# Expert lists: the compared places stored with four tiles innermost instead of eight

## The chip, the cores and the metric

The kernel runs on one core of one Trainium2 chip. The metric is the device time of one execution in microseconds (us); less is better. Three runs of the kernel before took 1474.82, 1474.82 and 1475.46 us, so the median is 1474.82 us. Engines are named as in the profile: PE (matrix multiplication), PEld (PE's loading of weights), DVE (vector), ACT (scalar activation), POOL (the general-purpose engine, which also issues indirect DMAs) and SP (which issues the other DMAs).

## The reference, cut to what matters

A tensor of 4 x 1024 tokens with 256 values each passes four sublayers, each as `x + layernorm(sublayer(layernorm(x)))`: a gated attention in groups of 64, a low-rank feed-forward, an attention with 16 heads whose weights are relu(scores), and a mixture of eight experts. Only the last one matters here:

```python
def _L1_ffn_ref(x, Wg, W1, b1, W2, b2):
    ...
    k = min(max(int(n * C / e), 1), n)          # 4096 * 2 / 8 = 1024 tokens an expert
    xt = x.reshape(n, h)
    S = jax.nn.sigmoid(xt @ Wg).T               # 8 x 4096 scores
    G, I = jax.lax.top_k(S, k)
    ex = xt[I]
    hid = jax.nn.gelu(jnp.einsum('ekh,ehf->ekf', ex, W1) + b1[:, None, :], approximate=False)
    out = (jnp.einsum('ekf,efh->ekh', hid, W2) + b2[:, None, :]) * G[..., None]
    new_x = jnp.zeros_like(xt).at[I.reshape(-1)].add(out.reshape(-1, h))
```

Each expert takes the 1024 tokens with its highest scores. The kernel has to turn the scores of an expert into a list of 1024 token numbers before it can gather the tokens.

## The kernel before, in words

The first three sublayers take the first 963 us and are left alone. What follows is the expert stage.

**Sizes.** P = 128 partitions; the 4096 tokens are NTILE = 32 tiles of 128, one token of each tile on each partition; an expert's list is NC = 8 chunks of 128; QT = 8 tiles are a quarter of the 32. An expert's 1024 tokens are worked on in two halves (`u` counts halves, 0 to 15) of 512.

**How a list is made** (class `List`; one object for each of the eight experts, steps run in this order). `Search` finds by bisection the score of the 1024th token. `sort` marks tokens above and at it; `rank` counts, with matmuls against triangular ones and scans, which place each chosen token has in the list, and splits the place into a chunk (`hi`) and a position within the chunk (`lo`, one bf16 number for each partition and tile; a token that is not chosen matches no position). `chunks` (L1934 to L1942) compares `hi` with the eight chunk numbers and makes `pair`: for each tile 16 columns, eight with the token's partition number and eight with its tile number. `places` (L1960 on) compares `lo` with the 128 positions: for a quarter of the tiles, one DVE instruction (L1966) writes for each partition, position and tile a bf16 one or zero into the tile `at`. The constant `each` holds the 128 positions in the form that `lo` has; before, it holds them once for each of the 32 tiles, so that the operand for a quarter is a slice of it. The first two quarters go to buffers of a pool (name `at`), the last two into space that the tile `x` no longer needs (`in_stored`, so their name in the profile is `x`). `collect` (L1976) then runs one matmul for each of the 32 tiles: weights are the 16 columns of `pair` of that tile, the moving operand is the 128 positions of that tile out of `at`. Before, the eight tiles of a quarter are innermost in `at`, so position p of one tile lies 8 elements, 16 bytes, behind position p - 1. Tile j adds into output partitions 32 (j % 4) to 32 (j % 4) + 15, so that four tiles in a row use four different groups of rows. ACT copies the sums (`listed`, L1985), and `gather` (L1988, L1990) adds the four groups with one more matmul, turns the result into the integers `idx`, and has POOL issue eight indirect DMAs (`got`, L2000) that fetch the tokens.

**What the experts do.** `turn` transposes the gathered tokens on PE (L2170). Experts 0, 1, 2 and 7 run plain matmuls (`feed_forward`, L2285), experts 3 to 6 a form with seven products in place of eight (`feed_forward_by_seven`, L2231, with additions on DVE at L2246, L2248, L2250, L2257 and L2260 between the products and weight sums on POOL at L2195). `project_back` (L2311) multiplies back; DVE adds the bias (L2326) and scales (L2327) into one of four buffers `y`, and POOL adds the rows to the result in memory with an indirect DMA (L2328), each of which waits until the one before has landed. The next pair of weight matrices is loaded by SP while an expert runs.

**What sets the order.** PE, DVE and ACT run in the order in which the program is written; nothing is reordered. The list of expert 0 is made first, with nothing beside it but short idle matmuls (L203). The steps of the other lists stand in an agenda and are taken one at a time between the matmuls of the experts (`go_on_with_lists`), when a counter of estimated time allows it; the estimates are constants in the code. So every list but the first has its 32 matmuls of `collect` in the middle of the matmuls of some expert.

Of the kernel before, what the change touches and what calls it, by code (L numbers as in the profile page):

```python
# [12 lines left out]
BF16 = mybir.dt.bfloat16  # L13
AF = mybir.ActivationFunctionType
# [5 lines left out]
P = 128  # L20
# [54 lines left out]
def kernel(  # L75
# [32 lines left out]
    nc = tc.nc  # L108
# [3 lines left out]
    NTILE = NT // P  # L112
# [109 lines left out]
    with ExitStack() as st1:  # L222
# [96 lines left out]
        for r in range(2):  # L319
            for j in range(4):  # L320
                at = 32 * j + HD * r
# [124 lines left out]
        wk = st1.enter_context(tc.tile_pool(name="l0", bufs=2))  # L446
# [12 lines left out]
        def later_counts():  # L459
            r = {}  # L460

            def count_int(name, shape, pattern, per_partition, tag=None, base=0):
                n_i = const.tile(shape, I32, tag=tag or name, name=name, bufs=3 if tag else 1)
                nc.gpsimd.iota(n_i, pattern=pattern, base=base, channel_multiplier=per_partition)
                return n_i

            def count(name, shape, pattern, per_partition, dtype, base=0):
                n_i = count_int(f"{name}_i", shape, pattern, per_partition, "whole", base)
                r[name] = const.tile(shape, dtype, name=name)
                nc.gpsimd.tensor_copy(r[name], n_i)  # L470

            count("count_p", [P, P], [[1, P]], 0, BF16, 1)
            count("count_c", [P, NC], [[1, NC]], 0, BF16)
            count("count_t", [P, NTILE], [[1, NTILE]], 0, BF16)
            count("in_tile", [P, 1], [[0, 1]], 1, F32)
            r["bits0"] = count_int("bits0", [P, NVAL], [[1, NVAL]], 0)
            r["ahead_i"] = count_int("ahead_i", [P, P], [[1, P]], -1, "whole")

            quads = r["quads"] = const.tile([P, 2 * NC], F32, name="quads")
            nc.gpsimd.tensor_tensor(quads, ident[:, 0 : 2 * NC], ident[:, 32 : 32 + 2 * NC], ALU.add)
            for q in (2, 3):
                nc.gpsimd.tensor_tensor(quads, quads, ident[:, 32 * q : 32 * q + 2 * NC], ALU.add)
            return r
# [525 lines left out]
        for t in range(NB):  # L1011
# [4 lines left out]
            if t == 0:  # L1016
                whole = later_counts()
            elif t == 1:
                mb1, all_b, upto_b, bits, fold = later_constants(whole)
                count_p, count_c, count_t, in_tile = (  # L1020
                    whole[name] for name in ("count_p", "count_c", "count_t", "in_tile")
                )
# [29 lines left out]
            while main:  # L1052
                on_pe(*main.pop(0))
                if not beside and hidden and len(main) % 2 == 0:
                    for step in (hidden.pop(0) for _ in range(min(2, len(hidden)))):
                        on_pe(*step)
                places = max(len(main) - len(hidden), 0) + 1
                for _ in range(-(-len(beside) // places)):
                    on_pe(*beside.pop(0))
# [44 lines left out]
    with ExitStack() as st3:  # L1104

        wts = st3.enter_context(tc.tile_pool(name="l1w", bufs=6))
        wk = st3.enter_context(tc.tile_pool(name="l1a", bufs=2))
# [557 lines left out]
        while True:  # L1665
# [7 lines left out]
            at = pe[0]  # L1673
# [76 lines left out]
    with ExitStack() as st4:  # L1750
        keep = st4.enter_context(tc.tile_pool(name="moe_keep", bufs=1))
# [27 lines left out]

        weights = [load_expert(0), load_expert(1)]  # L1780

        each = keep.tile([P, P, NTILE], BF16, name="each")
        behind_exp = mybir.DependencyInfo(mybir.DependencyClass.Sync, mybir.DependencyReason.DATA)
        whole = nc.scalar.activation(each, count_p.unsqueeze(2).to_broadcast([P, P, NTILE]), AF.Copy, scale=-1.0 / P)
        tc.add_manual_dep(whole.ins, state["exp"].ins.name, behind_exp, reason="the last scores go ahead")

        whole_c = keep.tile([P, NC], F32, name="whole_c")
# [9 lines left out]
        wk = st4.enter_context(tc.tile_pool(name="moe", bufs=2))  # L1797
        ps = st4.enter_context(tc.tile_pool(name="moe_ps", bufs=2, space=PSUM))
        QT = NTILE // 4
# [81 lines left out]
        def in_stored(half):  # L1881

            room = xs[ADDED - 1].rearrange("p j d -> p (j d)")[:, half * TB : (half + 1) * TB]
            return room.bitcast(BF16).rearrange("p (a b) -> p a b", b=QT)

        class List:

# [72 lines left out]
            def places(self, part):  # L1960
                js = slice(part * QT, (part + 1) * QT)
                if part < 2:
                    self.at[part] = wk.tile([P, P, QT], BF16, tag="at", name="at", bufs=2)
                else:
                    self.at[part] = in_stored(part - 2)
                nc.vector.tensor_tensor(  # L1966
                    self.at[part],
                    self.lo[:, js].unsqueeze(1).to_broadcast([P, P, QT]),
                    each[:, :, js],
                    ALU.is_equal,  # L1970
                )

            def collect(self, part):
                for j in range(part * QT, (part + 1) * QT):
                    u = 32 * (j % 4)
                    nc.tensor.matmul(  # L1976
                        parts[u : u + 2 * NC, 0:P],
                        lhsT=self.pair[:, j, :, :].rearrange("p v c -> p (v c)"),
                        rhs=self.at[part][:, :, j - part * QT],
                        start=(j < 4),  # L1980
                        stop=(j >= NTILE - 4),
                    )
                if part == 3:
                    self.listed = wk.tile([P, P], BF16, tag="listed", name="listed")
                    nc.scalar.copy(self.listed, parts[:, 0:P])  # L1985
# [443 lines left out]
```

## Time and profile before

| | us |
|---|---|
| median of three runs | 1474.82 |
| lowest, highest | 1474.82, 1475.46 |
| the profiled execution, its time | 1478.4 |
| the profiled execution, span of its instructions | 1476.6 |
| busy PE, DVE, ACT, POOL (of the span) | 1418.0, 868.6, 738.4, 531.3 |
| DVE compares of `places` (L1966), 32 | 20.6 busy |
| PE matmuls of `collect` (L1976), 256 | 17.8 busy |
| ACT writing the constant `each` (L1784), one | 3.60 |

The profiled execution is one execution on the chip with a record of each instruction; times of single instructions are from it. In a timeline row the first number is the start, the second how long the group was busy, then engine, line, operation, output <- inputs, partitions x elements and type, and in brackets how long the engine had been idle and what ended that. In a group's row the numbers behind the bar are busy time in all, mean ns of one instruction, then idle time ahead of it. Matmuls are pipelined, so one starts long before the one ahead of it ends: how many fit into a time is read from their starts. PEclk, the clock that the throttle granted to PE, is 1.00 in nearly all of the expert stage.

### The profile page before, as it was taken

How to read it: one execution, taken by the hardware profiler on the slowest of the kernel's cores; microseconds unless marked ns; L12 is line 12 of the kernel's file. 1: busy time of each engine (PE TensorE's matmuls, PEld its weight loads, DVE VectorE, ACT ScalarE, POOL GpSimd, SP SyncE). 2: the span in 40 equal slices, each digit the busy share in tenths (PEclk: the TensorE clock that was granted, in tenths of full speed). 3: DMA queues.
4: the chain of work that ended last, by engine and by line, in shares of the span. 5: the costliest groups of instructions: out<-in, count | busy, mean ns of one | idle time of the engine just before them, and what ended most of it. 6: DMA issues, size and time to landing. Idle time of an engine off the chain costs nothing. (4 is left out here: it accounts for less than half of the span.)

```text
span 1476.6 us, 26427 instructions
## 1 busy us (share of the span) xinstructions
PE 1418.0 (96%) x10392; PEld 861.1 (58%) x10392; DVE 868.6 (59%) x2134; ACT 738.4 (50%) x1013; POOL 531.3 (36%) x662
## 2 busy tenths in 40 slices
PE   8999999999899999999999999849999998999997
PEld 4666666667544545544555458527666665756674
DVE  5456655576554648565765677774536765355246
ACT  4244555444368887788778788422211232232142
POOL 4023231232352324342333123422344333553655
PEclk9999999999999999999999999969999999999999
DMA  8400000002643482456246430241333323343364
GB/s 221 138 1 1 1 1 1 1 0 83 203 122 97 122 249 76 146 163 195 83 119 209 135 87 19 90 122 22 101 73 80 75 65 54 73 101 58 73 167 132
DMA packets 104854, 138.76 MB, mean 94 GB/s; under 512 B 25470, under 2 KB 64795, under 8 KB 104603
## 3 DMA queue, kind: packets, MB, share of 16 engines
q1 hardware_dynamic: 74512, 81.75, 18.0%
q0 software_dynamic: 30160, 55.32, 16.1%
q8 instruction: 81, 1.33, 0.4%
q14 instruction: 43, 0.34, 0.1%
q10 hardware_dynamic: 58, 0.01, 0.0%
HBM read 75.29 MB, written 61.51 MB: 93 GB/s over the span
## 5 line engine op out<-in xcount | busy, mean ns | idle before, releaser
L1705 ACT ACTIVATE w<-sc 128x1024 f32<-128x1024 f32 x394 | 378.9, 1024 | 61.4 <-PE sc L1528 60.7
L1549 PE MATMUL po<-w,vaug 128*17 128x256 f32 (+1 forms) x4608 | 255.9, 358 | 0.9 <-DVE turned L1607 0.6
L2311 PE MATMUL py<-w,hid 128*128 128x256 f32 x1024 | 230.6, 383 | 3.3 <-DVE y L2326 3.3
L2311 PEld LDWEIGHTS py<-w,hid 128*128 128x128 f32 x1024 | 193.0, 191 | 33.8 <-issue 4.2
L1707 DVE TENSOR_SCALAR w<-sc 128x1024 f32<-128x1024 f32 x118 | 143.7, 1220 | 79.1 <-PE sc L1528 76.0
L1549 PEld LDWEIGHTS po<-w,vaug 128*17 128x17 f32 x4608 | 116.4, 97 | 117.2 <-issue 48.2
L1528 PE MATMUL sc<-q,kT 64*128 64x512 f32 (+1 forms) x1152 | 170.8, 404 | 2.9 <-ACT w L1705 1.5
L2328 POOL DMA_INDIRECT acc_d<-y,idx x56 | 88.8, 1585 | 171.1 <-issue 29.9
L1528 PEld LDWEIGHTS sc<-q,kT 64*128 64x128 f32 x1152 | 90.1, 185 | 84.1 <-issue 45.5
L2292 ACT ACTIVATE hid<-ph,mb 128x512 f32<-128x512 f32 (+1 forms) x72 | 45.8, 639 | 164.7 <-PE ph L2285 135.3
L2285 PE MATMUL ph<-xT,w 128*128 128x512 f32 (+1 forms) x288 | 114.8, 552 | 0.3 <-DVE xT L2176 0.3
L2000 POOL DMA_INDIRECT got<-tok_d,idx x64 | 66.3, 1037 | 77.9 <-DVE idx L1990 60.5
L2285 PEld LDWEIGHTS ph<-xT,w 128*128 128x128 f32 x288 | 52.6, 190 | 51.9 <-issue 48.9
L2326 DVE TENSOR_TENSOR y<-py,mb 128x256 f32<-128x256 f32 x56 | 23.6, 421 | 77.4 <-PE py L2311 50.5
L371 POOL DMA_DIRECT2D kT<-k_d x32 | 23.4, 732 | 117.0 <-PE sc L1528 53.9
L722 PE MATMUL pg<-nT,wh 128*128 128x512 f32 x128 | 60.8, 607 | 1.5 <-ACT nT L661 1.5
L848 PE MATMUL py<-wo,oT 128*128 128x256 f32 x256 | 61.6, 384 | 0.0
L738 PE MATMUL pv<-wh,nT 128*128 128x512 f32 x128 | 59.7, 592 | 0.0
L848 PEld LDWEIGHTS py<-wo,oT 128*128 128x128 f32 x256 | 47.5, 190 | 17.6 <-issue 11.0
L746 ACT ACTIVATE v<-v 128x512 f32<-128x512 f32 x32 | 20.2, 630 | 62.7 <-DVE v L745 62.7
L586 POOL TENSOR_TENSOR x<-x,y 128x1024 f32<-128x1024 f32 x13 | 30.6, 2355 | 56.4 <-ACT y L575 56.3
L1137 POOL TENSOR_TENSOR rsb<-veb,mhalf 128x1 f32<-128x1 f32 x30 | 19.7, 656 | 83.8 <-DVE veb L1136 83.8
(345 smaller groups left out, 2356.4 us busy)
## 6 DMA issues: line engine op xcount, KB each, us to landing
q<-q_d POOLq DMA_DIRECT2D x16, 1024.0 KB
kT<-k_d POOLq DMA_DIRECT2D x32, 512.0 KB
w<-in_L_ffn_W_dram SPq DMA_DIRECT2D x16, 1024.0 KB
k_d<-parts SPq DMA_DIRECT2D x48, 256.0 KB
q_d<-parts SPq DMA_DIRECT2D x48, 256.0 KB
acc_d<-logits SPq DMA_DIRECT2D x8, 512.0 KB
tok_d<-hg SPq DMA_DIRECT2D x30, 128.0 KB
x<-in_L_attn_x_dram SPq DMA_DIRECT2D x7, 512.0 KB
```

Source lines behind the costliest of these rows:

```text
L722: nc.tensor.matmul(pg, lhsT=wh[:, c, HID + e * P : HID + (e + 1) * P], rhs=d["nT"][:, c, :], start=(c == 0), stop=(c == DC - 1),)
L738: nc.tensor.matmul(pv, lhsT=d["nT"][:, c, i * P : (i + 1) * P], rhs=wh[:, c, 0:HID], start=(c == 0), stop=(c == DC - 1),)
L848: nc.tensor.matmul(py, lhsT=d["oT"][:, e, :], rhs=wo[:, e, :], start=(e == 0), stop=(e == EC - 1))
L1528: nc.tensor.matmul(sc[:, j, m * n : (m + 1) * n], lhsT=row["kT"][t, r][rows, u, (kt + m) * P : (kt + m + 1) * P], rhs=row["q"][qh, t][rows ...
L1549: nc.tensor.matmul(po[rows : rows + HD + 1, at : at + n], lhsT=row["v"][:, kt + m, HQ * t + 4 * r + 2 * u + j, :], rhs=w[:, j, (2 * m + pa ...
L1705: nc.scalar.activation(w, sc, AF.Relu)
L1707: nc.vector.tensor_scalar(w, sc, 0.0, None, ALU.max)
L2000: return nc.gpsimd.indirect_dma_start(out=dst, out_offset=None, in_=rows[:, :], in_offset=self.at_chunk(c), bounds_check=NT - 1, oob_is_er ...
L2285: nc.tensor.matmul(ph, lhsT=w1[:, c, f * P : (f + 1) * P], rhs=xT[u][:, c, h * n : (h + 1) * n], start=(c == 0), stop=(c == DC - 1),)
L2292: gelu = nc.scalar.activation(hid[:, f, h * n : (h + 1) * n], ph, AF.Gelu, bias=mb1[:, e * FC + f : e * FC + f + 1])
L2311: nc.tensor.matmul(py, lhsT=hid[:, f, i * P : (i + 1) * P], rhs=w2[:, f, :], start=(f == 0), stop=(f == FC - 1),)
L2328: scatter = nc.gpsimd.indirect_dma_start(out=acc_d[:, :], out_offset=lists[e].at_chunk(k), in_=y, in_offset=None, bounds_check=NT - 1, oob ...
```

## The change: what it does

The tile of a quarter is split into two halves of four tiles, one behind the other; in each half the four tiles are innermost. Position p of a tile now lies 4 elements, 8 bytes, behind position p - 1. The constant `each` holds every position four times instead of 32 times, and the compare uses it for both halves, by an operand with a step of zero. The count of instructions, their order on each engine and what they wait for stay as they are; the constant takes 1 KB in each partition in place of 8 KB. The same numbers are computed.

```diff
-        each = keep.tile([P, P, NTILE], BF16, name="each")
+        each = keep.tile([P, P, 4], BF16, name="each")
...
-        whole = nc.scalar.activation(each, count_p.unsqueeze(2).to_broadcast([P, P, NTILE]), AF.Copy, scale=-1.0 / P)
+        whole = nc.scalar.activation(each, count_p.unsqueeze(2).to_broadcast([P, P, 4]), AF.Copy, scale=-1.0 / P)
...
-            return room.bitcast(BF16).rearrange("p (a b) -> p a b", b=QT)
+            return room.bitcast(BF16).rearrange("p (h a b) -> p h a b", a=P, b=4)
...
-                    self.at[part] = wk.tile([P, P, QT], BF16, tag="at", name="at", bufs=2)
+                    self.at[part] = wk.tile([P, QT // 4, P, 4], BF16, tag="at", name="at", bufs=2)
...
                 nc.vector.tensor_tensor(
                     self.at[part],
-                    self.lo[:, js].unsqueeze(1).to_broadcast([P, P, QT]),
-                    each[:, :, js],
+                    self.lo[:, js].rearrange("p (h b) -> p h b", b=4).unsqueeze(2).to_broadcast([P, QT // 4, P, 4]),
+                    each.unsqueeze(1).to_broadcast([P, QT // 4, P, 4]),
                     ALU.is_equal,
                 )
...
-                        rhs=self.at[part][:, :, j - part * QT],
+                        rhs=self.at[part][:, j % QT // 4, :, j % 4],
```

## The prediction

> **What bounds the kernel now.** I read the table of stages first (one row per stretch, microseconds from the span's start; columns: length, busy time and instructions of PE, PEld, DVE, ACT, POOL, then granted clock, DMA share, GB/s), because the page's shares mix five stages and the change sits in the last one, the experts from 963 us on.
>
> ```profile
> 1040.00:1090.00 50.00, 50.00 (x200) 34.32 (x198) 28.74 (x89) 7.56 (x11) 16.60 (x12) 1.00 0.35 76
> 1090.00:1140.00 50.00, 50.00 (x239) 32.30 (x239) 23.85 (x68) 9.46 (x15) 24.90 (x21) 1.00 0.41 100
> 1190.00:1240.00 50.00, 46.15 (x213) 32.90 (x211) 26.14 (x52) 9.98 (x17) 21.43 (x17) 0.98 0.31 75
> 1300.00:1360.00 60.00, 59.82 (x272) 38.88 (x271) 29.40 (x63) 17.44 (x30) 27.44 (x21) 1.00 0.35 73
> ```
>
> The reader is to see the first busy column: PE has work all the time, DVE half of it. PE's gaps between 990 and 1445 us are 4.63 us before 1240.78, 3.35 us before 1390.75 and three under 0.4 us. So PE's instruction stream sets the end here. The chain of waits, followed back from the end, says the same and names the changed line three times (start, length, what):
>
> ```profile
> 1238.05 1.28 DVE at L1966 x2
> ...
> 1244.56 1.97 PE parts L1976 x29
> 1246.52 6.21 PE ph L2231 x14
> ...
> 1300.53 1.93 PE parts L1976 x31
> ...
> 1356.76 1.94 PE parts L1976 x32
> ```
>
> L1976 is `collect`: 32 matmuls per list that read the compared places; L1966 is `places`, the DVE compare that writes them. Next the groups of these lines by form (count, then busy us and mean ns of one), and the timeline around one `collect`:
>
> ```profile
> L1966 DVE TENSOR_TENSOR at<-lo,each 128x1024 bf16<-128x1024 bf16 x16 | 10.3, 682 | 0.0
> L1976 PE MATMUL parts<-at,pair 128*16 128x128 bf16 x128 | 8.8, 402 | 0.2 <-DVE at L1966 0.2
> L745 DVE TENSOR_TENSOR v<-pv,bhv 128x512 f32<-128x512 f32 x32 | 22.1, 690 | 27.2 <-PE pv L738 27.0
> L1549 PE MATMUL po<-w,vaug 128*17 128x256 f32 x3584 | 223.9, 383 | 0.7 <-DVE turned L1607 0.3 <-ACT w L1705 0.3
> ...
> 988.03 1.02 PE L203 MATMUL idle<-all_b 128*128 128x512 bf16 x4
> ...
> 1356.69 1.10 PE L1976 MATMUL parts<-at,pair 128*16 128x128 bf16 x16
> 1357.58 1.12 PE L1976 MATMUL parts<-x,pair 128*16 128x128 bf16 x16
> 1358.63 1.12 PE L2231 MATMUL ph<-xT,w 128*128 128x512 f32 x2
> ...
> 612.26 1.49 PE L1549 MATMUL po<-w,vaug 128*17 128x256 f32 x24
> ```
>
> The durations overlap, so starts are what to read. The four matmuls of tiles j % 4 write four groups of 32 output rows and start within 10 ns (1356.691, .694, .698, .701), the next four 0.21 us later: a list is eight waves of four. Four waves take 1357.58 - 1356.69 = 0.89 us, 0.2225 us each, for 128 columns: 1.74 ns a column. The contiguous bf16 matmuls of L203 take (1.02 - 0.38) / 3 = 0.213 us for 512 columns, 0.42 ns each. Packing four matmuls side by side is not what costs the factor of four: L1549 packs four of 256 f32 columns and needs (1.49 - 0.38) / 5 = 0.222 us a wave, what an unpacked 256-column f32 matmul also needs (16 of L2311 in 3.46 us, 0.216 us). What L1976 has and none of these has is the step: column p is read at p * 8 elements, 16 bytes on. So I read four times the contiguous price as the price of that step. Eight waves and the tail to the next matmul are 1358.63 - 1356.69 = 1.94 us a list.
>
> **The change, part by part.** Instruction order and waits are the same on all five engines; three things differ.
>
> (1) *The constant `each`* is written as 128x512 instead of 128x4096. Before: 3599 ns on ACT at 963.44. After, by an ACT row of 512 elements (L746, 630 ns): some 0.63 us, 3.0 us less. Cover: ACT has loaded its next table by 968.55 us, then idles 17.9 us for L1976; its reader on DVE comes at 983.20. Worth 0. If that cover were gone it would still be a gain.
>
> (2) *The compare* keeps 1024 elements and its bf16 operands; only the order is 2 x 128 x 4 instead of 128 x 8, and the constant is read contiguously instead of in runs of 16 bytes every 64. Its 682 ns equal the 690 ns of a 512-element f32 operation, so it handles two elements where that handles one. Best case: nothing to gain, since runs of 16 bytes already go at that rate. Worst: one element at a time, 690 + 512 x 1.04 ns (slope from 421 ns at 256 f32, L2326, to 690 at 512) = 1.22 us, 0.54 us more each. I take 0, the nearest row being the same instruction with rows twice as long; the upper end is a rival. The Trainium skill, "Vector Engine (DVE) Microarchitecture Reference", Measured stream behaviour, says that a port keeps its rate while elements come in runs of at least two adjacent 4-byte words on an 8-byte boundary; four bf16 are just that, so by it the compare stays at 0.68 us too; no row of this profile has rows so short.
>
> (3) *The matmuls' step* becomes 8 bytes. No row shows a PE read with that step, so I bound it: from below by the contiguous bf16 read, 0.42 ns a column, from above by today's 1.74 ns (nothing gained). Nothing shows a reason for a loss; the output and the weights are as before. If 16 bytes is one fetch a column and two columns now share a fetch, a column costs half, 0.83 ns, and a wave 128 x 0.83 = 0.107 us less. I take that: halving the step halves the memory covered, and the result lies between both ends. A wave is then 0.116 us; the weight loads of L1976 (mean 101 ns) go beside the wave before and hide only just; at a full-rate wave (0.2225 - 128 x 1.25 ns = 0.06 us) they would be the floor.
>
> Per list 8 x 0.107 = 0.85 us less PE time. For lists 1 to 7 (1029.9, 1090.3, 1114.3, 1194.0, 1244.5, 1300.5, 1356.7 us) PE is followed by the next `ph` matmuls without a gap, so it all counts: 7 x 0.85 = 5.95. List 0 is DVE's: its four compares come 0.60 us apart, and only the two waves after the last one (985.74 us, `listed` at 986.46) are open: 2 x 0.107 = 0.21.
>
> What is late next? `idx` of each list comes from PE and DVE and starts POOL's gathers (POOL waited 18.9 us for it at 1203.30, 2.9 us at 1365.98), and from them the serial chain of scatters (one per 4.5 us) that ends in the two PE gaps. Both chains start behind a `collect`, so gaps move along and neither grows. The stores at the end hang on the last scatter, also moved.
>
> Sum: -(5.95 + 0.21) = -6.2 us, against 1478.4 us of the profiled execution (span 1476.6, 1.8 around it), 0.42%. The median, 1474.82, lies 3.6 us below that execution; a saving in PE work carries over as it is: 1474.8 - 6.2 = **1468.6 us**. Own range 1467 to 1470.5 (a tenth of it lost or gained; weight loads as floor).
>
> A rule weighed: the Trainium skill, "SBUF — State Buffer", Specifications and the note on lines in Door 1, says that memory lines are 16 bytes, that two hits per line are needed for full bandwidth, and that eight bf16 is how far one can step for free. By the last part today's step would be free; the 1.74 ns above disagree. By the first part four innermost give two hits, thus the full rate and the fast rival below.
>
> **The rivals.**
> - *Full rate.* Two columns a fetch are enough to hide it: a column goes to 0.42 ns, a list saves 8 x 128 x 1.25 ns = 1.28 us; 7 x 1.28 + 0.32 = 9.3: 1465.5 us. Against: weight loads of 101 ns a wave would hold it at 8 x 0.12 = 0.97 a list, 1467.8.
> - *The step is not the unit.* Every column that does not touch its neighbour costs a fetch, at 8 bytes as at 16: no change, 1474.8 us. For it: 8 bytes in some 1.7 ns is just what L203 (four bf16) and L2311 (two f32, 0.84 ns a column) get, so the fetch may be 8 bytes wide. The pair granule of the skill's DVE page, cited above, would speak for it, if PE's port were alike; no run shows that.
> - *PE is not what ends last.* The scatter that lands at 1237.25 and frees `y` for DVE ends PE's 4.63 us gap. If it kept its time, lists 1 to 4 would save nothing: 3 x 0.85 + 0.21 = 2.8, 1472.1 us. Against: POOL's own 18.9 us wait for `idx` at its root.
> - *Slower: DVE loses the two at a time.* With rows of four, each compare takes 1.22 us. List 0: 4 x 0.54 = 2.15 open. Lists 5 and 7: two compares each stand before the subtraction that PE waits for (chain, 1238.05; 1352.06): 2 x 1.07 = 2.15. Together +4.3 with no gain on PE: 1479.1 us; up to 1483 if all twelve compares of lists 5 to 7 count (2.15 + 12 x 0.54 = 8.6). It decides once a compare costs more than about 0.54 x 6.2 / 4.3 = 0.8 us extra with the gain, or any 0.4 us without.
>
> **How the numbers follow.** Half price 0.52, full rate 0.14, no change on PE 0.15, chain elsewhere 0.05, slower DVE 0.14. About 0.2% (2.9 us) is what a measurement tells from no change. Half price and full rate are faster: 0.66. No change and the chain (-0.19%) are the same: 0.20. Slower: 0.14. The range reaches from the full rate to no change with the runs' spread of 0.6 us: 1465.3 to 1475.4, leaving out the DVE case.
>
> **What would show it.** `each` at about 0.63 us; compares at 0.68 us; a `collect` from first matmul to the next `ph` of about 1.1 us instead of 1.94, single matmuls near 0.29 us instead of 0.40; PE's two gaps unchanged; the start of the last `collect` some 5.3 us earlier. I am wrong if waves still start 0.22 us apart, if compares exceed 0.75 us, or if the waves shrink and one of the two gaps grows by as much.

## The result, and the profile after

The changed kernel takes 1469.39 us (median of six runs, 1468.98 to 1469.76), the kernel before 1474.87 us beside it (six runs, 1474.66 to 1475.46): a ratio of 0.9963 with a 95% interval of 0.9951 to 0.9975, 5.5 us less. The forecast was 1468.6 us. Two executions are left out of the medians below as disturbed: one of the kernel before, of 5138.84 us, and one of the kernel with eight buffers, of 1500.65 us at a mean granted clock of 0.934.

The profiled execution of the changed kernel took 1469.39 us with a span of 1467.3. First its lines L1784 and L1976 by source line (count, then shortest, median and longest in ns, first and last start in us, shape), then the groups by form (count, busy us, mean ns of one, idle time ahead of it):

```profile
L1784 ACT ACTIVATE each<-count_p x1: 612/612/612, 964.4 to 964.4; 128x512 bf16<-128x512 bf16 x1
...
L1976 PEld LDWEIGHTS <-pair x256: 85/108/116, 984.7 to 1354.3; 128*16 128x16 bf16 x128
...
L1976 PE MATMUL parts<-at,pair x128: 272/294/308, 984.9 to 1353.9; 128*16 128x128 bf16 x128
```

```profile
L1966 DVE TENSOR_TENSOR at<-lo,each 128x1024 bf16<-128x1024 bf16 x16 | 10.3, 683 | 0.0
```

The constant fell from 3599 to 612 ns, the compare stayed at 683 ns, and the median matmul of `collect` out of `at` went from 406 to 294 ns. The timeline of PE (start, busy us, engine, line, group; in brackets the idle time ahead and what ended it) shows the one gap that is left, and then the last list:

```profile
1232.55 1.02 PE L2231 MATMUL ph<-xT,w 128*128 128x512 f32 x2
1238.95 2.08 PE L2231 MATMUL ph<-x,w 128*128 128x512 f32 x2 [5.38 <-DVE hid L2248]
1240.82 1.91 PE L2231 MATMUL ph<-xT,x 128*128 128x512 f32 x2
...
1353.59 0.63 PE L1976 MATMUL parts<-at,pair 128*16 128x128 bf16 x16
1354.04 0.67 PE L1976 MATMUL parts<-x,pair 128*16 128x128 bf16 x16
1354.63 0.70 PE L2231 MATMUL ph<-xT,w 128*128 128x512 f32 x1
```

From the first matmul of the last list to the next `ph` it is 1354.63 - 1353.59 = 1.04 us, where it was 1.94. Its waves of four start at 0, 0.096, 0.211, 0.326, 0.441, 0.557, 0.674 and 0.790 us: from the second wave on they are 0.116 us apart. (Read in the same way, those of before are 0.227 us apart.) Seven of the eight lists have this form, 1.025 to 1.057 us against 1.92 to 1.96. The chain of waits names the line again, with half the length:

```profile
1228.55 6.85 DMA acc_d<-y,idx
...
1236.22 1.28 DVE at L1966 x2
...
1238.95 3.78 PE ph L2231 x4
1242.73 1.06 PE parts L1976 x28
...
1353.66 1.04 PE parts L1976 x28
```

And the table of stretches (length; busy us and count of PE, PEld, DVE, ACT, POOL; granted clock, DMA share, GB/s) is that of before, with PE still at work all the time but for the stretch with the gap:

```profile
1040.00:1090.00 50.00, 50.00 (x199) 34.24 (x197) 29.02 (x89) 7.56 (x11) 16.45 (x12) 1.00 0.33 75
...
1233.50:1239.00 5.50, 0.12 (x2) 0.05 (x1) 3.26 (x6) 0.69 (x1) 1.59 (x1) 0.91 0.41 74
1239.00:1243.00 4.00, 4.00 (x17) 1.46 (x21) 2.81 (x5) 1.44 (x2) 1.61 (x1) 0.50 0.18 22
...
1243.00:1249.00 6.00, 6.00 (x39) 2.94 (x28) 2.52 (x4) 1.61 (x4) 1.54 (x1) 0.85 0.35 41
```

The rows at 1239 and 1243 show what the gap costs beyond itself: behind 5.38 us without work the granted clock is 0.50 for 4 us and 0.85 for 6 more, and two `ph` matmuls take 1.87 us from start to start, where ahead of the gap they take 0.86. That would be 4 x 0.50 + 6 x 0.15 = 2.9 us of clock. But the list at 1242.66 lies in it and still takes its 1.06 us, so its share, 1.06 x 0.50 = 0.5, is not lost, and an estimate of 2.4 us is left. The Trainium skill, "TensorE: Matmul & The Clock Gate", Part 1, says that PE's clock falls to half after an idle window and comes back once PE has been busy for some time; these rows agree.

**Where the time went between the two profiled executions.** From the first `idx` (L1990) to the last instruction it was 489.57 us before and is 479.49 after, 10.1 less, more than the medians differ by. Seven lists give 7 x 0.91 = 6.4. The kernel before had a second gap, and its clock fell behind each of the two (of before: the second gap in the timeline of PE, then the stretches behind both gaps):

```profile
1390.75 12.31 PE L2311 MATMUL py<-w,hid 128*128 128x256 f32 x48 [3.35 <-DVE y L2326]
```

```profile
1240.70:1244.70 4.00, 3.92 (x9) 1.28 (x13) 2.71 (x6) 1.44 (x2) 1.56 (x1) 0.50 0.14 22
1244.70:1250.00 5.30, 5.30 (x41) 2.41 (x34) 1.94 (x3) 1.57 (x3) 1.54 (x1) 0.96 0.39 38
...
1390.70:1394.70 4.00, 3.95 (x12) 3.26 (x13) 1.13 (x3) 0.00 (x0) 3.04 (x2) 0.65 0.31 33
1394.70:1400.00 5.30, 5.30 (x25) 4.62 (x24) 1.14 (x3) 0.00 (x0) 1.62 (x2) 0.94 0.38 36
```

The second gap and its clock, 3.35 + 4 x 0.35 + 5.3 x 0.06 = 5.1 us, are not there after. The first gap was 4.63 us and is 5.38 here. Its clock loss, less the part in which the list ran, was 4 x 0.50 + 5.3 x 0.04 - 0.3 = 1.9 us and is 2.4. So 1.3 us are taken back. 6.4 + 5.1 - 1.3 = 10.2. Half of what the two profiles show is therefore no work of the change, unless the second gap belongs to the kernel before; the first experiment asks that.

### The profile page after: what moved, and what is told of

Read it like the earlier page. It is cut to its first block, busy times and chain, and to the rows that moved or that the text cites. A ratio compares the mean times of both kernels' runs of the same rounds, so it can differ in the third digit from the quotient of the medians.

```text
span 1467.3 us, 26427 instructions
## 1 busy us (share of the span) xinstructions
PE 1410.2 (96%) x10392; PEld 859.9 (59%) x10392; DVE 869.7 (59%) x2134; ACT 735.0 (50%) x1013; POOL 531.3 (36%) x662
## 5 line engine op out<-in xcount | busy, mean ns | idle before, releaser
L2231 PE MATMUL ph<-xT,w 128*128 128x512 f32 x96 | 50.3, 606 | 0.0
```

The lines of the kernel that those rows point to most:

```text
L2231: nc.tensor.matmul(bank, lhsT=a[:, f * P : (f + 1) * P], rhs=b, start=start, stop=stop, skip_group_check=not start)
```

## The experiments

Two theories of the price of a column stood against each other. The first: each matmul pays for every new 16 bytes of memory that it touches, so 8 bytes of step halve it, 4 quarter it, 32 cost as much as 16. The rival: the four matmuls side by side share a way to memory (or their weight loads set the pace, 0.116 us a wave being close to the 108 ns of a load), so that the price hangs on their number. Beside these: whether the constant alone is worth anything, what a compare without its rate of two would have cost, and whether the gaps follow from the change.

**The kernel before, profiled once more** (no edit)

> The kernel before, a second profiled execution. The first one stood 3.6 us above its median and had a PE gap of 3.35 us before 1390.75 us that the changed kernel's profile does not have. If that gap belongs to the kernel, it is here again and the profiled time is near 1478; if it was an event of that one execution, PE runs through the multiplication back of expert 6 without a gap, and the profiled time is near 1475. Collects 1.92 to 1.96 us, the gap before the lists' fifth collect near 4.6 us either way.

It took 1473.4 us (span 1471.6), beside a median of 1475.19 (19 runs, 1473.35 to 1478.26). Its timeline of PE, the gap ahead of list 5 and the multiplication back of expert 6, in which the second gap lay:

```profile
1241.67 2.07 PE L2231 MATMUL ph<-x,w 128*128 128x512 f32 x2 [4.25 <-DVE hid L2248]
...
1377.17 18.08 PE L2311 MATMUL py<-w,hid 128*128 128x256 f32 x83
```

83 matmuls follow each other where the first profile had 3.35 us of nothing: the second gap belonged to that one execution, and its 5.1 us are more than the 3.6 us by which that execution lay above the median. The gap ahead of list 5 is there each time, but its length is not fixed. From the first `idx` to the end it is 483.36 us here, 6.2 less than in the first profile, of which that gap with its clock is 5.1.

**The constant alone**

```diff
-        each = keep.tile([P, P, NTILE], BF16, name="each")
+        each = keep.tile([P, P, 8], BF16, name="each")
...
-                    each[:, :, js],
+                    each,
```

> The kernel before with one part of the change alone: the constant shrunk to eight copies, places still eight innermost. Theory (all of the gain is the matmuls' step): the constant takes about 1.05 us on ACT instead of 3.6, nothing waits for it, collects stay at 1.92 us or more, time 1474.9, same as before. Rival (the smaller constant or the 7 KB that move give some of it): 1470 to 1473.

1475.37 us (10 runs, 1473.72 to 1477.1), ratio 1.0005 (0.9996 to 1.0015). By source line:

```profile
L1784 ACT ACTIVATE each<-count_p x1: 1038/1038/1038, 965.0 to 965.0; 128x1024 bf16<-128x1024 bf16 x1
...
L1976 PE MATMUL parts<-at,pair x128: 385/406/420, 985.5 to 1360.1; 128*16 128x128 bf16 x128
```

2.6 us less on ACT are worth nothing: they lie in ACT's idle time. With the compares at 683 ns as before, the gain is the matmuls'.

**Two tiles innermost: a step of 4 bytes** (the edits here, in the next experiment and in that on `y` are shown against the changed kernel; the ratios are all to the kernel before)

```diff
-        each = keep.tile([P, P, 4], BF16, name="each")
+        each = keep.tile([P, P, 2], BF16, name="each")
...
-                    self.at[part] = wk.tile([P, QT // 4, P, 4], BF16, tag="at", name="at", bufs=2)
+                    self.at[part] = wk.tile([P, QT // 2, P, 2], BF16, tag="at", name="at", bufs=2)
...
-                        rhs=self.at[part][:, j % QT // 4, :, j % 4],
+                        rhs=self.at[part][:, j % QT // 2, :, j % 2],
```

> Two tiles innermost, a step of 4 bytes, the constant with two copies. Theory (a column costs one fetch of a 16-byte line divided by the columns in it): column 0.42 ns, a single matmul record near 0.22 us instead of 0.29, but waves held near 0.10 us by the weight loads of 0.10 us. Rival (after the change the weight loads are already the floor and the read is already at full rate): the same records, 0.29 us, and waves of 0.116. On DVE rows are one 4-byte word: if pairs of words are needed, compares go from 0.68 to some 1.04 us, which costs list 0 four times 0.36 and lists 5 and 7 0.72 each, time about 1472; if not, 0.68 us and 1469.

1465.92 us (1463.99 to 1467.86, 4 runs), ratio 0.9947 (0.9930 to 0.9963). Timeline of PE, then two groups by form:

```profile
1348.97 0.41 PE L1976 MATMUL parts<-at,pair 128*16 128x128 bf16 x16
1349.21 0.40 PE L1976 MATMUL parts<-x,pair 128*16 128x128 bf16 x16
1349.54 0.70 PE L2231 MATMUL ph<-xT,w 128*128 128x512 f32 x1
```

```profile
L1966 DVE TENSOR_TENSOR at<-lo,each 128x1024 bf16<-128x1024 bf16 x16 | 10.3, 683 | 0.0
...
L1976 PEld LDWEIGHTS <-pair 128*16 128x16 bf16 x256 | 4.0, 90 | 8.0 <-issue 7.2 <-DVE pair L1942 0.8
```

A list takes 0.57 us, a wave 0.058: a quarter of the price at 16 bytes. The weight loads last 90 ns each and do not hold back waves of 0.058 us, so they were not what set the 0.116 us of the changed kernel. The expectation had waves of 0.10 us, held by the loads, and 1469 us; both were too high. Seven lists of 0.60 instead of 1.035 us in the mean, and 0.1 at list 0, make 3.2 us less than the changed kernel; the medians differ by 3.5. One list, that behind the gap, began at a granted clock of 0.50:

```profile
1239.28 0.57 PE L1976 MATMUL parts<-at,pair 128*16 128x128 bf16 x16
1239.67 0.41 PE L1976 MATMUL parts<-x,pair 128*16 128x128 bf16 x16
```

Its first half took 1239.67 - 1239.28 = 0.39 us, where the list above took 1349.21 - 1348.97 = 0.24; from its second wave on, the waves start 0.107 us apart. At this step the clock counts.

The compare keeps its 683 ns when `lo` comes in rows of two elements, one 4-byte word. The same row is read again for each position there, and the constant and the result lie contiguous, so this says nothing of rows of two that lie apart.

**Positions one behind the other: a step of 2 bytes** (the constant holds every position once)

```diff
-                    self.at[part] = wk.tile([P, QT // 4, P, 4], BF16, tag="at", name="at", bufs=2)
+                    self.at[part] = wk.tile([P, QT, P], BF16, tag="at", name="at", bufs=2)
...
-                    self.lo[:, js].rearrange("p (h b) -> p h b", b=4).unsqueeze(2).to_broadcast([P, QT // 4, P, 4]),
-                    each.unsqueeze(1).to_broadcast([P, QT // 4, P, 4]),
+                    self.lo[:, js].unsqueeze(2).to_broadcast([P, QT, P]),
+                    each.unsqueeze(1).to_broadcast([P, QT, P]),
```

> Positions of one tile side by side (step of 2 bytes), the constant once; DVE's other operand is then one element read again and again. PE: full rate by every theory, so a wave shows the floor that weight loads set, about 0.10 us; a collect 0.95 us. DVE: one element at a time, compares 1.22 us instead of 0.68. Priced as the prediction's slower rival: list 0 pays 4 x 0.54, lists 5 and 7 pay 1.07 each, so 4.3 us over the changed kernel less 0.5 for PE: 1473; up to 1477 if all twelve compares of lists 5 to 7 count. If DVE keeps 0.68 us: 1469.

1473.91 us (10 runs, 1472.6 to 1477.7), ratio 0.9995 (0.9985 to 1.0005): the same as before. Group by form, then timeline of PE:

```profile
L1966 DVE TENSOR_TENSOR at<-lo,each 128x1024 bf16<-128x1024 bf16 x16 | 18.8, 1219 | 0.0
```

```profile
1245.32 0.40 PE L1976 MATMUL parts<-at,pair 128*16 128x128 bf16 x16
1245.54 0.40 PE L1976 MATMUL parts<-x,pair 128*16 128x128 bf16 x16
1245.87 1.12 PE L2231 MATMUL ph<-xT,w 128*128 128x512 f32 x2
```

The matmuls gain nothing more (0.056 us a wave: that is the contiguous rate), but the compare, with one of its operands repeating a single element along the innermost run, takes 1219 ns, the time that the prediction worked out for one element at a time. Against two tiles innermost, which has the same matmuls within 0.02 us a list, it costs 1473.91 - 1465.92 = 8.0 us. The prediction's bounds for this were 4.3 us (the open compares) and 8.6 us (all twelve compares of lists 5 to 7); its upper one is the nearer. Beside the profile with two innermost, list 0 takes 2.2 us more from its first compare to `idx`. Lists 4, 6 and 7 each wait 0.64 us for their last compare in the middle of `collect`, which the lower bound has not in it and the upper one only for lists 6 and 7. PE waits 0.95 us for a subtraction ahead of each of lists 6 and 7, instead of 0.18 us ahead of list 7 alone, and the gap ahead of list 5 is 6.18 us instead of 4.98. That is 2.2 + 1.9 + 1.7 + 1.2 = 7.0 of the 8.0 us.

**All 32 matmuls on one group of rows**, none beside another, with a step of 16 bytes (kernel before) and of 8 (changed kernel)

```diff
-                    u = 32 * (j % 4)
+                    u = 0
...
-                        start=(j < 4),
-                        stop=(j >= NTILE - 4),
+                        start=(j == 0),
+                        stop=(j == NTILE - 1),
```

> The kernel before with all 32 matmuls of a collect on the same group of 32 output rows, so that they run one after the other instead of four side by side; step 16 bytes as before, the sums are the same. Theory A (a fetch takes its time in each stream by itself): each matmul still needs 0.21 us, 32 of them 6.9 us and more, a collect about 7.1 us, the time 35 to 41 us longer, some 1513. Theory B (the four streams share one read path that serves one line at a time, which is why four together took four times): alone a stream reads a column in 0.42 ns, matmuls come every 0.06 to 0.11 us (weight loads), a collect 1.9 to 3.5 us, time 1475 to 1486.

> The same on the changed kernel, step 8 bytes. Theory A with the line of 16 bytes: matmuls every 0.107 to 0.116 us, a collect about 3.6 us, the time some 19 us over the changed kernel, 1488. Theory A with the weight loads as the floor and a full-rate read: also near 0.11 us, but single records of 0.22 us instead of 0.28. Theory B: as in the run with 16 bytes, 1.9 to 3.5 us, no shorter than that one.

1532.53 us and 1490.0 us, one run of each, beside a median of 1475.55 (5 runs) for the kernel before. Timelines of PE, the kernel with 16 bytes first, then that with 8:

```profile
1104.92 3.79 PE L1976 MATMUL parts<-at,pair 128*16 128x128 bf16 x16
1108.54 3.81 PE L1976 MATMUL parts<-x,pair 128*16 128x128 bf16 x16
1112.27 1.22 PE L2285 MATMUL ph<-xT,w 128*128 128x512 f32 x1
```

```profile
1096.28 2.01 PE L1976 MATMUL parts<-at,pair 128*16 128x128 bf16 x16
1098.11 2.03 PE L1976 MATMUL parts<-x,pair 128*16 128x128 bf16 x16
1100.07 1.13 PE L2285 MATMUL ph<-xT,w 128*128 128x512 f32 x2
```

One matmul alone takes (1108.54 - 1104.92) / 16 = 0.226 us and (1098.11 - 1096.28) / 16 = 0.114 us: as long as four side by side. The price belongs to the stream and the rival falls; packing four hides three quarters of it. The kernel with 8 bytes came out near its expected 1488. That with 16 came out some 20 us later than expected. Its table of stretches around one list (1037.25 to 1044.60) shows most of that:

```profile
1037.00:1041.00 4.00, 4.00 (x18) 1.83 (x18) 0.00 (x0) 0.69 (x1) 0.00 (x0) 1.00 0.03 4
1041.00:1044.60 3.60, 3.60 (x17) 1.54 (x14) 0.00 (x0) 0.00 (x0) 0.00 (x0) 0.55 0.00 0
1044.60:1048.00 3.40, 3.40 (x5) 1.32 (x5) 0.00 (x0) 0.27 (x1) 0.00 (x0) 0.50 0.00 0
```

From the middle of such a list on the clock is 0.55 and then 0.50. The list itself does not notice: its matmuls start 0.227 us apart in its first half and in its second. (The second half, 1044.60 - 1040.86 = 3.74 us, is longer than the first, 3.61, only by the tail to the next matmul; with 8 bytes, at a clock of 1.00, the halves differ in the same way, 1.83 and 1.96.) The `ph` matmuls behind the list do notice. In the 8 us behind each of the seven lists the granted clock is 0.77, 0.74, 0.78, 0.67, 0.72, 0.85 and 0.71, by which 14.1 us are lost. 7 x (7.35 - 1.94) = 37.9 for the lists, 14.1 for the clock and 5.0 for list 0 (8.86 us from first compare to `idx` instead of 3.87) make 57.0, which is what was measured (1532.53 - 1475.55). Why the clock falls there, with PE busy all the time by its records, was not tried. With 8 bytes, where a list lasts 3.79 us, the clock stays at 1.00 through the lists and behind them, but for the list behind the gap; so either the length or the slower read may be the cause.

**A step of 32 bytes** (against the kernel before; lines are one later; the constant holds eight copies, and three quarters instead of two go to the pool)

```diff
-                    self.at[part] = wk.tile([P, P, QT], BF16, tag="at", name="at", bufs=2)
+                    self.at[part] = wk.tile([P, P, 2 * QT], BF16, tag="at", name="at", bufs=3)[:, :, 0:QT]
```

> Eight tiles innermost with eight unused elements behind them, a step of 32 bytes; the constant with eight copies. Theory (one fetch for each column that touches a new line): waves 0.2225 us as at 16 bytes, records 0.40 us, collects 1.94 us, time 1475. Rival (the price grows with the distance): waves 0.44 us, a collect 3.7 us, time 1488. Compares 0.68 us if DVE may hop between rows of 16 bytes on writing.

1475.78 us (one run, beside the same 1475.55). Timeline of PE:

```profile
1303.14 1.10 PE L1977 MATMUL parts<-at,pair 128*16 128x128 bf16 x16
1304.05 0.66 PE L1977 MATMUL parts<-x,pair 128*16 128x128 bf16 x8
1304.51 0.66 PE L1977 MATMUL parts<-at,pair 128*16 128x128 bf16 x8
1305.10 0.70 PE L2232 MATMUL ph<-xT,w 128*128 128x512 f32 x1
```

1305.10 - 1303.14 = 1.96 us a list, 0.232 us a wave: within 3% of 16 bytes. Twice the distance costs hardly more, so a column at 16 bytes already pays the full price of one fetch. The compares, which now write rows of 16 bytes with 16 bytes between them, keep 685 ns.

**Eight buffers of `y` instead of four** (L2325 of the changed kernel)

```diff
-                y = wk.tile([P, D], F32, tag="y", name="y", bufs=4)
+                y = wk.tile([P, D], F32, tag="y", name="y", bufs=8)
```

> The changed kernel with eight buffers for y instead of four. Before list 5's collect PE idles 5.38 us because DVE's y waits for a scatter to free a buffer. Theory (the gap is that buffer, and POOL's chain of scatters has room to catch up before the next list's gathers): the gap goes, 4 to 5 us gained, 1464 to 1465.5. Rival (the scatters are late anyway and the gathers of list 5 stand behind them): the gap moves to PE's wait for the gathered tokens of expert 5, 1469.

1464.6, 1460.77 and 1461.57 us, ratio 0.9905 (0.9881 to 0.9929) to the kernel before; the median of the three is 7.8 us below the 1469.39 of the changed kernel. The timeline of PE where the gap was:

```profile
1236.18 1.02 PE L2231 MATMUL ph<-xT,w 128*128 128x512 f32 x2
1237.09 1.13 PE L2231 MATMUL ph<-x,w 128*128 128x512 f32 x2
1238.05 1.02 PE L2231 MATMUL ph<-xT,x 128*128 128x512 f32 x2
1239.00 0.63 PE L1976 MATMUL parts<-at,pair 128*16 128x128 bf16 x16
```

The gap is gone, and none came in its place: with a free buffer DVE adds into `y` without waiting for the scatter, the compares behind it come at 1234.35, and PE goes on. So this scatter did hold the changed kernel up here, as the prediction's chain had it. From the `idx` of list 4 to that of list 5 it takes 43.02 us instead of 50.88, 7.9 less, where 4 to 5 were expected. The expectation counted the gap alone; the clock behind it, 2.4 us, comes on top: 5.38 + 2.4 = 7.8. The four added buffers take 4 KB in each partition, of the 7 KB that the smaller constant gives back. Eight buffers on the kernel before were not run.

**The changed kernel once more, and both steps together** (two tiles innermost and eight buffers)

> The changed kernel once more, beside the two-innermost kernels on one chip, for the size of its gain and for the gap before list 5's collect. That gap was 4.63 and 4.25 us in the two profiles of before and 5.38 us in the first profile of after. Theory (it varies from execution to execution with the landing of one scatter, and takes nothing of the gain for good): between 4.2 and 5.5 us here, collects 1.03 us, time 0.9955 to 0.997 of before. Rival (the gap grows by what the collects save): 5.4 us again and above every profile of before.

> Two tiles innermost and eight buffers for y together. If the two gains do not touch each other: a collect of 0.57 us, no gap before list 5's collect, 8 us less than with two innermost alone, 1458, 0.988 of before. If the steps saved by one were waits of the other: 1461 to 1463.

The changed kernel: 1468.56 us (5 runs, 1466.71 to 1469.19) against 1475.27 (9 runs), ratio 0.9951 (0.9937 to 0.9964). Its profile has lists of 1.036 to 1.056 us, 4.83 us of gap ahead of list 5 (4.25 and 4.63 in the two profiles of before, 5.38 in the first of after) and no second gap. Two more profiles bear on whether the gap grows by what the lists save. The kernels with only a smaller constant and with a step of 32 bytes have lists as long as before (1.92 to 1.97 us), and this gap:

```profile
1243.49 2.08 PE L2231 MATMUL ph<-x,w 128*128 128x512 f32 x2 [5.41 <-DVE hid L2248]
...
1243.46 2.08 PE L2232 MATMUL ph<-x,w 128*128 128x512 f32 x2 [5.40 <-DVE hid L2249]
```

So it is 4.25 to 5.41 us with long lists, and 4.83, 4.98 (two innermost) and 5.38 with short ones: it varies from execution to execution, and nothing shows that the change made it longer.

Both steps together: 1459.33 us (4 runs, 1457.98 to 1460.94), ratio 0.9889 (0.9874 to 0.9904). That is 9.2 us below the changed kernel that ran beside it, where 7.9 (the buffers, between two `idx`) and 2.6 to 3.8 (the step: 9.3 us below the kernel before, against 5.5 and 6.7) would make 10.5 to 11.7. The gains nearly add, and this version is the fastest here.

## Why the prediction was right

- *PE bounds the expert stage.* Right. What PE saved at the lists agrees with what the time fell by: 7 x 0.91 + 0.22 = 6.6 us by the records, 5.5 (interval 3.7 to 7.2) and 6.7 us (5.3 to 9.3) by the medians of two comparisons.
- *(1) The constant is worth nothing.* Right, and shown alone: 612 ns (estimated 630), and 1.0005 with only the constant made smaller.
- *(2) The compare stays.* Right: 683 ns, with rows of four and even of two. The rule of the Trainium skill that stood beside it, "Vector Engine (DVE) Microarchitecture Reference", Measured stream behaviour, agrees for rows of four (683 ns); rows of two, one word long and read again and again, keep the rate as well. The slower rival did not come, but its price did where it was provoked: 1219 ns against 1.22 us.
- *(3) Half the price.* Right in mechanism. A wave was forecast at 0.116 us and measured 0.116; a list was to save 0.85 us and saved 0.89 to 0.93. That the 0.116 was met so closely is partly luck, for two small errors cancel in it. The wave of before was read as 0.2225 us from two group starts, with the shorter first wave in it, and is 0.227 us from the second wave on. And half of the 1.74 ns a column is 0.87, not 0.83; with it the forecast would have been 0.111 us a wave. The saving itself was 0.227 - 0.116 = 0.111 us a wave, 0.89 a list. List 0 was to give 0.21 and gave 0.22 (3.87 to 3.65 us from first compare to `idx`).
- *The weight loads as a floor.* Wrong, without effect here: loads of 90 ns stand beside waves of 0.058 us. With it falls the time of 1467.8 us that the prediction gave for a full-rate read held up by loads.
- *Full rate with two columns a fetch.* Did not come: 0.90 ns a column, twice the contiguous price. Four columns a fetch reached it (0.45 ns); three were not tried. The rival's saving of 1.25 ns a column does not fit the prediction's own 1.74 and 0.42, which lie 1.32 apart; the step of 4 bytes saved 1.93 - 0.57 = 1.36 us a list. The rule of the Trainium skill behind this rival, "SBUF — State Buffer", Specifications, has the 16 bytes right, as the equal price at 16 and 32 shows, but two hits a line are not full bandwidth for this read.
- *The step is not the unit (a fetch of 8 bytes).* Fell: it would have left the waves at 0.2225 us.
- *"Both chains start behind a `collect`, so gaps move along and neither grows."* Half wrong. The gap of 3.35 us was no property of the kernel and did not move along; neither the second profile of before nor the two of after have it. The gap ahead of list 5 did move along: 4.83 and 5.38 us after lie within the 4.25 to 5.41 of the four profiles with long lists. The rival that the scatter in front of it would keep its time fell as well: by the chains of waits it landed at 1237.23 us before and at 1235.40 after, counted from the first `idx` 2.6 us earlier of the 3.6 that four lists save.
- *The last `collect` starts 5.3 us earlier.* In the profiles it starts 3.1 us earlier (1353.59 against 1356.69), and 4.1 counted from the first compare of list 0, ahead of which the two executions already differ by 1.0. List 5's gap with its clock, 1.3 us more in this one profile, is the difference to 5.3. The other 5 us by which the profiles differ come behind it, from the gap that was only in the first profile of before.
- *The median carries the saving of PE over, though the profiled execution was 3.6 us long.* Right, and partly by luck: the prediction did not know why that execution was longer. It had the second gap and the clock behind it, which are no work of PE.

## What to carry to other kernels

Where many matmuls read an operand with a step, price a column by the 16-byte lines that it newly touches, then lay the operand out so that four or more columns share a line (bf16 with a step of at most 4 bytes here). Look for the layout that still gives the engine that writes it full rows (here two elements were enough and a single repeated one was not). A short gap on PE costs more than itself: add the clock behind it before deciding that it isn't worth a buffer. And profile the kernel before twice: a gap that is in one execution only is no term of a sum.

## What the runs showed of the hardware

- Time of a column of a bf16 read on PE, by step (wave or matmul spacing / 128): 0.44 ns at 2 bytes, 0.45 at 4, 0.90 at 8, 1.77 at 16, 1.81 at 32. That is about 1.77 ns for each new 16 bytes, with the contiguous price of 0.44 at a clock of 1.00 as a floor.
- The same for one stream alone as for each of four side by side (0.226 and 0.114 us a matmul alone, 0.227 and 0.116 a wave of four).
- The price of a step of 8 or 16 bytes stands in wall time, not in clocks: with 16 bytes, matmuls on one group of rows started 0.227 us apart at a granted clock of 1.00 and of 0.55 alike, and the changed kernel's list at 1242.66, begun at a clock of 0.50, took 1.06 us like the others. With 4 bytes, near the floor, it follows the clock: a wave took 0.107 us at 0.50 and 0.058 at 1.00.
- A gap of 3.4 to 5.4 us on PE was followed by a clock of 0.50 to 0.65 for 4 us, worth an estimated 1.4 to 2.4 us more. With 16 bytes and one group of rows, 7.35 us of matmuls without a gap brought the clock down to 0.55 and 0.50 as well; 3.79 us of them with 8 bytes did not.
